# Local attention: keys turned by 32x32 blocks on VectorE and regrouped through DRAM

## The chip, the cores and the metric

The kernel runs on one core of a Trainium2 chip. A core has five engines that work side by side, each through its own queue in order: TensorE (PE in the profile, with its weight loads as PEld), VectorE (DVE), ScalarE (ACT), GpSimd (POOL) and SyncE (SP), which here only issues DMA transfers. Engines wait for each other on semaphores. The metric is the device time of one launch in microseconds.

## The reference, cut to what matters

A transformer of two parts, all in float32. The first part has an attention with relative positions over 16 sequences of 256 tokens, and then six local layers; the second a causal attention and a mixture of experts. The change touches only the attention of the six local layers (16 heads of 64, windows of 32 tokens, each window looking at itself and the one before it):

```python
qkv = x @ Wqkv
q, k, v = split(qkv, 3)                 # then per head
q = l2norm(q) * qs
k = l2norm(k) * ksc
q = q * cos * scale + rotate_half(q) * sin * scale
k = k * cos * inv + rotate_half(k) * sin * inv
sim = einsum('bhwie,bhwje->bhwij', bq, bk2) * 8.0
sim = where(mask, -finfo.max, sim)
attn = softmax(sim, -1)
out = einsum('bhwij,bhwje->bhwie', attn, bv2)
return out @ Wo
```

Since the length of a query is one number for its row and head, dividing by it may come before the rotation, after it, or as a factor of the logits.

## The kernel before

One launch runs four stages in turn: relative attention (`relative_attention`), the six local layers (`local_layers`), causal attention and experts. In the local layers the tokens are cut into tiles of 128 (two per sequence, 32 per layer, 192 in all, `m` in the code). The loop at the end of `local_layers` makes 201 passes; in a pass `at` it issues each entry `(behind, step, ...)` of the table `STEPS` for the tile `at - behind`. So several tiles are in flight, each at a different step, and the order of the table is the order of the instructions: `env.in_order(first)` chains all instructions of PE, ACT, DVE and POOL to the order in which they were written, engine by engine. SP is left out of that, and its transfers are put where the scheduler wants them. Tiles come from pools with a fixed number of buffers (`one`, `two`, `ftwo`, ...); a new tile waits until the last reader of the old one in that buffer has finished. Accumulators are `big` (two buffers of 1024 columns) and `small` (four of 512).

The path of one tile through the steps that matter here:

- `project(m, j)` (L1129; j = 0 is the queries, 1 the keys): two matmuls into a `big` (L1135), squares by ACT (L1146), products with the rotary tables by DVE (L1147, and L1151 on the swapped halves), and their sum by POOL (L1156). It is called for the keys and then for the queries.
- `lengths` (L1160): DVE adds up the squares of queries and keys (L1163).
- `normalise` (L1166): POOL bounds the sums from below (L1169), `power` (L1024) takes the inverse root (ACT L1026, L1027; POOL L1028 to L1031), and POOL multiplies the queries and the keys by it (L1174, twice).
- `turn(m, j)` (L1176): PE turns queries, and in another step keys, 8 blocks of 128x128 each (L1192), ACT copies the result into `a_qT` or `a_kT` (L1193).
- `logits` (L1195): 64 small matmuls into a `big` (L1207); DVE adds the band that masks (L1215) and takes the maximum of each row and head (L1221).
- `exponentials` (L1225): ACT, one head at a time, in three lots of 6, 4 and 6 heads (L1228, each with a read of its accumulator).
- `sums` (L1236): DVE's reciprocal (L1239) and POOL's product with it (L1240). `turn_weights`: DVE turns the weights by 32x32 blocks (L1245).
- `gather` (L1250): matmuls with the tokens (L1260), copied out by ACT (L1268, L1278) and DVE (L1276). `output`: 16 matmuls (L1285) and DVE's sum with the input (L1292).

The feed-forward half of a layer runs once in four passes, for four tiles together (`group`): statistics on DVE (L1316, L1317) with POOL's f_ve behind them (L1319), scaling on DVE (L1331), DVE's product L1374 and sum L1404, POOL's L1397, and their matmuls (L1350, L1366, L1382). `fetch` and `inputs` load a sequence three and two passes ahead (a_xt, L1037 to L1039, and a_xm, L1078 and L1079). POOL also clears edges of fresh tiles (memsets L1040, L1080, L1185).

Of the kernel before, what the change touches and what calls it, by code (L numbers as in the profile page):

```python
# [35 lines left out]
NEG = -1e30  # L36
# [898 lines left out]
def local_layers(tc, I, xa, xb, env):  # L935
# [14 lines left out]
    with ExitStack() as octx:  # L950
# [35 lines left out]
        fou = octx.enter_context(tc.tile_pool(name="a_fou", bufs=4))  # L986

# [15 lines left out]
        x_of, xs_of, kT_of, ffn = {}, {}, {}, {}  # L1003

# [124 lines left out]
        def project(m, j):  # L1129

            i, b, t = where(m)
            ta, tb = tabs[i]["qk"[j]]
            ps = big()
            for c in range(2):
                T.matmul(  # L1135
                    ps[:, c * 512 : (c + 1) * 512],
                    lhsT=xs_of[i, b][:, t, 0:P],
                    rhs=weights[i]["qk"[j]][:, c * 512 : (c + 1) * 512],
                    start=True,
                    stop=True,  # L1140
                )
            ps3 = ps.rearrange("p (h d) -> p h d", h=H)
            u = two.tile([P, H, DH], F32, name=f"a_u{j}")
            r = one.tile([P, H, DH], F32, name=f"a_r{j}")
            sq = one.tile([P, H, DH], F32, name=f"a_sq{j}")
            A.activation(sq, ps3, AF.Square)  # L1146
            V.tensor_mul(u, ps3, bcast(ta[:, t].unsqueeze(1), (P, H, DH)))  # L1147
            swapped = bass.AP(
                ps.tensor, ps.offset + HF, [list(ps.ap[0]), [DH, H], [-HF, 2], [1, HF]]
            )  # L1150
            V.tensor_mul(  # L1151
                r.rearrange("p h (s e) -> p h s e", s=2),
                swapped,
                bcast(tb[:, t].rearrange("p (s e) -> p s e", s=2).unsqueeze(1), (P, H, 2, HF)),
            )
            G.tensor_add(u, u, r)  # L1156
            st[m]["u", j], st[m]["sq", j] = u, sq
            ahead(m, "qk"[j])

        def lengths(m):  # L1160
            ss = two.tile([P, 2, H], F32, name="a_ss")
            for j in range(2):
                V.tensor_reduce(ss[:, j], st[m]["sq", j], AX.X, ALU.add)  # L1163
            st[m]["ss"] = ss

        def normalise(m):  # L1166

            ss = st[m]["ss"]
            G.tensor_scalar_max(ss, ss, 1e-24)  # L1169
            y = two.tile([P, 2, H], F32, name="a_y")  # L1170
            power(ss, y)
            for j in range(2):
                u = st[m]["u", j]
                G.tensor_mul(u, u, bcast(y[:, j].unsqueeze(2), (P, H, DH)))  # L1174

        def turn(m, j):  # L1176

            i, b, t = where(m)
            if j == 0:
                dst = two.tile([P, NP, P], F32, name="a_qT")  # L1180
                st[m]["qT"] = dst
            else:
                if t == 0:
                    kT_of[i, b] = two.tile([P, NP, WIN + S], F32, name="a_kT")
                    G.memset(kT_of[i, b][:, :, 0:WIN], 0.0)  # L1185
                dst = kT_of[i, b][:, :, WIN + t * P : WIN + (t + 1) * P]
            u = st[m]["u", j].rearrange("p h d -> p (h d)")
            for c in range(2):
                ps = small().rearrange("p (c s) -> p c s", c=4)
                for k in range(4):  # L1190
                    o = (4 * c + k) * P
                    T.transpose(ps[:, k, :], u[:, o : o + P], ident)  # L1192
                A.copy(dst[:, 4 * c : 4 * c + 4], ps)  # L1193

        def logits(m):  # L1195
# [7 lines left out]
            for c in range(NP):  # L1203
                for win in range(4):
                    for e in range(2):
                        q0 = WIN * win
                        T.matmul(  # L1207
                            ps[q0 : q0 + WIN, e, c, :],
                            lhsT=qT[DH * e : DH * (e + 1), c, q0 : q0 + WIN],
                            rhs=kT[DH * e : DH * (e + 1), c, t * P + q0 : t * P + q0 + 2 * WIN],  # L1210
                            start=True,
                            stop=True,
                        )
# [7 lines left out]
            V.tensor_reduce(nb, pr, AX.X, ALU.max, negate=True)  # L1221
            den = two.tile([P, H], F32, name="a_den")
            st[m].update(pr=pr, nb=nb, den=den)

        def exponentials(m, h0, h1):  # L1225
            s_ = st[m]
            for h in range(h0, h1):
# [4 lines left out]
                    bias=s_["nb"][:, h : h + 1],  # L1232
                    accum_out=s_["den"][:, h : h + 1],
# [8 lines left out]
        def turn_weights(m):  # L1242

            pT = two.tile([P, H, 2, WIN], F32, name="a_pT")
# [5 lines left out]
        def gather(m):  # L1250
# [21 lines left out]
            for win in (2, 3):  # L1272
                o = g[:, :, WIN * win : WIN * (win + 1)]
                p_ = ps[win].rearrange("p (h q) -> p h q", h=H)
                if win == 2:
                    V.tensor_copy(o, p_)  # L1276
                else:
                    A.copy(o, p_)  # L1278
# [121 lines left out]
        def f_add(i, g):  # L1400
# [7 lines left out]

        STEPS = (
            (2, logits),  # L1410
            (3, sums),
            (0, project, 1),
            (7, group(f_turn)),
            (0, project, 0),
            (3, turn_weights),
            (2, exponentials, 10, 16),
            (1, turn, 0),
            (-2, inputs),
            (4, output),
            (2, exponentials, 0, 4),  # L1420
            (5, group(f_stats)),
            (1, turn, 1),
# [3 lines left out]
            (0, lengths),  # L1426
            (0, fold),
            (5, group(f_power)),
            (3, gather),
            (0, normalise),  # L1430
# [21 lines left out]
        for at in range(N + 9):  # L1452
            for behind, step, *args in STEPS:
                if 0 <= at - behind < N:
# [585 lines left out]
```

## Time and profile before

| what | value |
|---|---|
| time, median of 3 runs | 4092.95 us (4092.0 to 4095.04) |
| span of the profiled execution | 4095.9 us |
| granted TensorE clock over the span | 0.990 |
| PE, DVE, ACT, POOL busy | 98%, 81%, 81%, 68% |
| local layers, about | 720 to 3600 us |
| L1192, turns of queries and keys | 3072 matmuls, 403.0 us busy |
| L1156 / L1174 on POOL, 384 each | 2368 / 1902 ns each |
| L1163 on DVE, 384 | 1201 ns each |

The profile gives one execution, whose own time is not listed beside the runs; its span, from the first to the last instruction, stands for it. A group's line reads: line, engine, operation, output <- inputs, shapes, count, then busy us and mean ns, then the idle time of the engine just before these instructions and who ended it. A line of waits reads: who waited, for whom, us in total, times, longest. A timeline line reads: start us, length us, engine, line, operation, output <- inputs, count, and in brackets the idle time before it. Idle time of an engine that does not set the end costs nothing.

### The profile page before, as it was taken

How to read it: one execution, taken by the hardware profiler on the slowest of the kernel's cores; microseconds unless marked ns; L12 is line 12 of the kernel's file. 1: busy time of each engine (PE TensorE's matmuls, PEld its weight loads, DVE VectorE, ACT ScalarE, POOL GpSimd, SP SyncE). 2: the span in 40 equal slices, each digit the busy share in tenths (PEclk: the TensorE clock that was granted, in tenths of full speed). 3: DMA queues.
4: the chain of work that ended last, by engine and by line, in shares of the span. 5: the costliest groups of instructions: out<-in, count | busy, mean ns of one | idle time of the engine just before them, and what ended most of it. 6: DMA issues, size and time to landing. Idle time of an engine off the chain costs nothing.

```text
span 4095.9 us, 141197 instructions
## 1 busy us (share of the span) xinstructions
PE 4006.0 (98%) x57676; PEld 2910.4 (71%) x57676; DVE 3299.3 (81%) x6445; ACT 3298.4 (81%) x11432; POOL 2774.8 (68%) x3334
## 2 busy tenths in 40 slices
PE   8999999899999999999999999999999999989999
PEld 6888887566777677677767767776776777756666
DVE  5666665788888888888888888888888888869985
ACT  4777776688888888888888888888888888879983
POOL 3333332888888888888888888888888888723221
PEclk9999999899999999999999999999999999999999
DMA  2111112100000000000000000000000000000000
GB/s 70 33 35 35 32 37 60 26 16 20 21 24 19 15 20 20 25 21 20 18 26 15 20 20 21 25 19 15 21 15 25 16 15 15 9 4 2 2 8 22
DMA packets 181812, 90.00 MB, mean 22 GB/s; under 512 B 142493, under 2 KB 173220, under 8 KB 181164
## 3 DMA queue, kind: packets, MB, share of 16 engines
q1 hardware_dynamic: 181164, 80.97, 7.5%
q8 instruction: 455, 7.45, 0.8%
q14 instruction: 193, 1.58, 0.1%
HBM read 38.49 MB, written 6.31 MB: 11 GB/s over the span
## 4 chain that ended last, share of the span: by engine, by line
PE 72%; POOL 6%; ACT 3%; issue 2%; DVE 1%; POOLq 0%; DMA 0%; DVEq 0%; ACTq 0%; SPq 0%
PE small L1285 16%; PE big L1135 13%; PE small L1192 8%; PE big L1260 7%; PE big L1207 5%; PE small L1382 3%; PE small L1366 3%; PE small L1350 3%; PE small L1627 3%; POOL a_u L1174 3%; PE big L1583 3%; PE small L1260 2%; PE small L1643 1%; ACT a_g L1268 1%; POOL a_u L1156 1%
## 5 line engine op out<-in xcount | busy, mean ns | idle before, releaser
L1228 ACT ACTIVATE a_pr<-a_pr,a_nb 128x64 f32<-128x64 f32 x3072 | 1024.1, 338 | 5.8 <-DVE a_nb L1221 5.8
L1156 POOL TENSOR_TENSOR a_u<-a_u,a_r 128x1024 f32<-128x1024 f32 x384 | 900.7, 2368 | 30.7 <-DVE a_r L1151 25.6
L1174 POOL TENSOR_TENSOR a_u<-a_u,a_y 128x1024 f32<-128x1024 f32 x384 | 722.5, 1902 | 15.0
L1285 PE MATMUL small<-a_vo,a_g 128*128 128x128 f32 x6144 | 719.0, 275 | 1.6 <-DVE c_st L1500 1.6
L1285 PEld LDWEIGHTS small<-a_vo,a_g 128*128 128x128 f32 x6144 | 702.5, 192 | 2.6 <-ACT a_g L1278 2.5
L1146 ACT ACTIVATE a_sq<-big 128x1024 f32<-128x1024 f32 x384 | 390.9, 1020 | 263.0 <-PE big L1135 262.7
L1228 ACT ACTIVATION_READ_ACCUMULATOR a_pr<-a_pr,a_nb 128x1 f32 x3072 | 587.8, 191 | 0.0
L1192 PEld LDWEIGHTS small<-ident,a_u 128*128 128x128 f32 x3072 | 350.9, 141 | 141.6 <-POOL a_u L1174 90.4
L1163 DVE TENSOR_REDUCE a_ss<-a_sq 128x16 f32<-128x1024 f32 x384 | 445.9, 1201 | 0.0
L1192 PE MATMUL small<-ident,a_u 128*128 128x128 f32 x3072 | 403.0, 274 | 24.5 <-POOL a_u L1174 21.1
L1135 PE MATMUL big<-w_k,a_xs 128*128 128x512 f32 x768 | 382.9, 621 | 4.6 <-ACT a_xs L1075 4.2
L1240 POOL TENSOR_TENSOR a_pr<-a_pr,a_rd 128x1024 f32<-128x1024 f32 x192 | 365.6, 1904 | 13.0 <-DVE a_rd L1239 13.0
L1135 PE MATMUL big<-w_q,a_xs 128*128 128x512 f32 x768 | 362.0, 594 | 0.6 <-DVE a_r L1151 0.6
L1207 PEld LDWEIGHTS big<-a_kT,a_qT 64*32 64x32 f32 x24576 | 262.7, 105 | 123.4 <-issue 63.8
L1215 DVE TENSOR_TENSOR a_pr<-big,w_band 128x1024 f32<-128x1024 f32 x192 | 234.9, 1223 | 108.6 <-PE big L1207 108.6
L1147 DVE TENSOR_TENSOR a_u<-big,a_tak 128x1024 f32<-128x1024 f32 x192 | 235.1, 1225 | 86.9 <-ACT a_sq L1146 86.9
L1207 PE MATMUL big<-a_kT,a_qT 64*32 64x64 f32 x24576 | 294.6, 226 | 4.7 <-POOL a_kT L1185 4.4
L558 DVE CUSTOM_DVE_ANT_0 r_lg<-big,r_rq 128x256 f32<-128x256 f32 x512 | 186.7, 421 | 132.3 <-PE big L547 81.2
L1268 ACT COPY a_g<-big 128x1024 f32<-128x1024 f32 x192 | 193.6, 1008 | 107.0 <-PE small L1260 106.5
L1135 PEld LDWEIGHTS big<-w_q,a_xs 128*128 128x128 f32 x768 | 142.8, 191 | 163.6 <-issue 126.8
L574 ACT ACTIVATE r_lg<-r_lg,r_nb 128x256 f32<-128x256 f32 x512 | 254.6, 511 | 5.0 <-DVE r_nb L558 5.0
L1609 ACT ACTIVATE c_lg<-c_lg,c_nb 128x256 f32<-128x256 f32 x512 | 255.5, 513 | 0.1
(292 smaller groups left out, 9252.8 us busy)
## 6 DMA issues: line engine op xcount, KB each, us to landing
a_xm<-a_xt SPq DMA_DIRECT2D x96, 96.0 KB
r_dk<-r_rowsk SPq DMA_DIRECT2D x64, 128.0 KB
r_dq<-r_rowsq SPq DMA_DIRECT2D x64, 128.0 KB
f_xt<-xa SPq DMA_DIRECT2D x96, 64.0 KB
f_xt<-xa SPq DMA_DIRECT2D x96, 63.5 KB
a_xt<-xa SPq DMA_DIRECT2D x80, 64.0 KB
a_xt<-xa SPq DMA_DIRECT2D x80, 63.5 KB
w_k<-in_L_ffn_Wqkv_dram SPq DMA_DIRECT2D x6, 512.0 KB
```

What stands on the lines that cost most here:

```text
L1135: T.matmul(ps[:, c * 512 : (c + 1) * 512], lhsT=xs_of[i, b][:, t, 0:P], rhs=weights[i]["qk"[j]][:, c * 512 : (c + 1) * 512], start=True, s ...
L1146: A.activation(sq, ps3, AF.Square)
L1156: G.tensor_add(u, u, r)
L1163: V.tensor_reduce(ss[:, j], st[m]["sq", j], AX.X, ALU.add)
L1174: G.tensor_mul(u, u, bcast(y[:, j].unsqueeze(2), (P, H, DH)))
L1192: T.transpose(ps[:, k, :], u[:, o : o + P], ident)
L1207: T.matmul(ps[q0 : q0 + WIN, e, c, :], lhsT=qT[DH * e : DH * (e + 1), c, q0 : q0 + WIN], rhs=kT[DH * e : DH * (e + 1), c, t * P + q0 : t * ...
L1228: A.activation(s_["pr"][:, h], s_["pr"][:, h], AF.Exp, bias=s_["nb"][:, h : h + 1], accum_out=s_["den"][:, h : h + 1],)
L1240: G.tensor_mul(s_["pr"], s_["pr"], bcast(rd.unsqueeze(2), (P, H, DH)))
L1260: T.matmul(ps[win], lhsT=x[r, t, :], rhs=pT[r, :, o, :], start=(o == 0), stop=(o == 1),)
L1285: T.matmul(ps[:, 0:D], lhsT=st[m]["g"][:, h, :], rhs=weights[i]["vo"][:, h // 2, h % 2, :], start=(h == 0), stop=(h == H - 1),)
L1609: A.activation(lg[:, j], lg[:, j], AF.Exp, bias=nb[:, j : j + 1], scale=-1.0, accum_out=st[b, lc]["den"][:, h : h + 1],)
```

## The change

Keys are no longer turned by PE. DVE turns them by 32x32 blocks (`block_turn`), four DMA transfers write the blocks to DRAM in the order that the logits want, and one reads them back into `a_kT`, now laid out by windows (`keys`). `project` is cut in two: `project` makes the matmuls and squares, `rope` the products with the tables and POOL's sum. The queries are not normalised before the logits: their inverse length multiplies the negated maximum (a DVE multiply in `logits`) and goes into the exponentials as a scale per row. The lengths are taken one side at a time: those of the keys right after their projection, those of the queries at the end of the pass, after POOL has added the two halves of the squares, so that DVE reduces 512 columns instead of 1024. `powers(n)` takes the inverse root for the keys of tile n and the queries of tile n - 1 together. In `gather` ACT takes over the copy that DVE made. `a_pT` has one buffer instead of two. The mask's value is -1e18 instead of -1e30. In the changed program's order DVE's reduction of the queries' squares is L1184, POOL's half add L1182, the turn of the keys L1217.

```diff
--- before
+++ after
-NEG = -1e30
+NEG = -1e18
...
+        held = octx.enter_context(tc.tile_pool(name="a_held", bufs=2, space=DRAM))
...
         def project(m, j):
             i, b, t = where(m)
-            ta, tb = tabs[i]["qk"[j]]
             ps = big()
             for c in range(2):
                 T.matmul(
...
                     start=True,
                     stop=True,
                 )
-            ps3 = ps.rearrange("p (h d) -> p h d", h=H)
+            sq = one.tile([P, H, DH], F32, name=f"a_sq{j}")
+            A.activation(sq, ps.rearrange("p (h d) -> p h d", h=H), AF.Square)
+            st[m]["ps", j], st[m]["sq", j] = ps, sq
+            ahead(m, "qk"[j])
+        def rope(m, j):
+            i, b, t = where(m)
+            ta, tb = tabs[i]["qk"[j]]
+            ps = st[m].pop(("ps", j))
             u = two.tile([P, H, DH], F32, name=f"a_u{j}")
             r = one.tile([P, H, DH], F32, name=f"a_r{j}")
-            sq = one.tile([P, H, DH], F32, name=f"a_sq{j}")
-            A.activation(sq, ps3, AF.Square)
-            V.tensor_mul(u, ps3, bcast(ta[:, t].unsqueeze(1), (P, H, DH)))
+            V.tensor_mul(
+                u,
+                ps.rearrange("p (h d) -> p h d", h=H),
+                bcast(ta[:, t].unsqueeze(1), (P, H, DH)),
+            )
             swapped = bass.AP(
                 ps.tensor, ps.offset + HF, [list(ps.ap[0]), [DH, H], [-HF, 2], [1, HF]]
             )
...
                 bcast(tb[:, t].rearrange("p (s e) -> p s e", s=2).unsqueeze(1), (P, H, 2, HF)),
             )
             G.tensor_add(u, u, r)
-            st[m]["u", j], st[m]["sq", j] = u, sq
-            ahead(m, "qk"[j])
-        def lengths(m):
-            ss = two.tile([P, 2, H], F32, name="a_ss")
-            for j in range(2):
-                V.tensor_reduce(ss[:, j], st[m]["sq", j], AX.X, ALU.add)
-            st[m]["ss"] = ss
+            st[m]["u", j] = u
+        def lengths(m, j):
+            n = m + 1 - j
+            if n not in ss_of:
+                ss_of[n] = two.tile([P, 2, H], F32, name="a_ss")
+                if n in (0, N):
+                    G.memset(ss_of[n][:, n // N], 1.0)
+            sq = st[m].pop(("sq", j))
+            if j == 0:
+                G.tensor_add(sq[:, :, 0:HF], sq[:, :, 0:HF], sq[:, :, HF:DH])
+                sq = sq[:, :, 0:HF]
+            V.tensor_reduce(ss_of[n][:, j], sq, AX.X, ALU.add)
+        def powers(n):
+            ss = ss_of.pop(n)
+            G.tensor_scalar_max(ss, ss, 1e-24)
+            y_of[n] = two.tile([P, 2, H], F32, name="a_y")
+            power(ss, y_of[n])
         def normalise(m):
-            ss = st[m]["ss"]
-            G.tensor_scalar_max(ss, ss, 1e-24)
-            y = two.tile([P, 2, H], F32, name="a_y")
-            power(ss, y)
-            for j in range(2):
-                u = st[m]["u", j]
-                G.tensor_mul(u, u, bcast(y[:, j].unsqueeze(2), (P, H, DH)))
-        def turn(m, j):
-            i, b, t = where(m)
-            if j == 0:
-                dst = two.tile([P, NP, P], F32, name="a_qT")
-                st[m]["qT"] = dst
-            else:
-                if t == 0:
-                    kT_of[i, b] = two.tile([P, NP, WIN + S], F32, name="a_kT")
-                    G.memset(kT_of[i, b][:, :, 0:WIN], 0.0)
-                dst = kT_of[i, b][:, :, WIN + t * P : WIN + (t + 1) * P]
-            u = st[m]["u", j].rearrange("p h d -> p (h d)")
+            u = st[m]["u", 1]
+            G.tensor_mul(u, u, bcast(y_of[m][:, 1].unsqueeze(2), (P, H, DH)))
+        def turn(m):
+            dst = two.tile([P, NP, P], F32, name="a_qT")
+            st[m]["qT"] = dst
+            u = st[m]["u", 0].rearrange("p h d -> p (h d)")
             for c in range(2):
                 ps = small().rearrange("p (c s) -> p c s", c=4)
                 for k in range(4):
                     o = (4 * c + k) * P
                     T.transpose(ps[:, k, :], u[:, o : o + P], ident)
                 A.copy(dst[:, 4 * c : 4 * c + 4], ps)
+        def block_turn(m):
+            u = st[m]["u", 1]
+            ub = one.tile([P, 4, NP * WIN], F32, name="a_ub")
+            V.transpose(
+                ub.rearrange("p e x -> p (e x)"),
+                bass.AP(u.tensor, u.offset, [list(u.ap[0]), [HF, 4], [P, NP], [1, HF]]),
+            )
+            o = st[m]["held"] = held.tile([P, 4, NP * WIN], F32, name="a_rows")
+            for w in range(4):
+                nc.sync.dma_start(
+                    o.rearrange("(e d) w x -> d e w x", e=4)[:, :, w],
+                    ub[WIN * w : WIN * (w + 1)],
+                )
+        def keys(m):
+            i, b, t = where(m)
+            if t == 0:
+                kT_of[i, b] = two.tile([P, 1 + 4 * NT, NP * WIN], F32, name="a_kT")
+                G.memset(kT_of[i, b][:, 0], 0.0)
+            nc.sync.dma_start(kT_of[i, b][:, 1 + 4 * t : 5 + 4 * t], st[m].pop("held"))
         def logits(m):
...
                         T.matmul(
                             ps[q0 : q0 + WIN, e, c, :],
                             lhsT=qT[DH * e : DH * (e + 1), c, q0 : q0 + WIN],
-                            rhs=kT[DH * e : DH * (e + 1), c, t * P + q0 : t * P + q0 + 2 * WIN],
+                            rhs=kT[
+                                DH * e : DH * (e + 1),
+                                4 * t + win : 4 * t + win + 2,
+                                WIN * c : WIN * (c + 1),
+                            ],
                             start=True,
                             stop=True,
                         )
...
             )
             nb = two.tile([P, H], F32, name="a_nb")
             V.tensor_reduce(nb, pr, AX.X, ALU.max, negate=True)
+            V.tensor_mul(nb, nb, y_of[m + 1][:, 0])
             den = two.tile([P, H], F32, name="a_den")
             st[m].update(pr=pr, nb=nb, den=den)
...
                     s_["pr"][:, h],
                     AF.Exp,
                     bias=s_["nb"][:, h : h + 1],
+                    scale=y_of[m + 1][:, 0, h : h + 1],
                     accum_out=s_["den"][:, h : h + 1],
                 )
...
         def turn_weights(m):
-            pT = two.tile([P, H, 2, WIN], F32, name="a_pT")
+            pT = one.tile([P, H, 2, WIN], F32, name="a_pT")
             V.transpose(
                 pT.rearrange("p h o q -> p (h o q)"), st[m]["pr"].rearrange("p h k -> p (h k)")
             )
...
             for win in (2, 3):
                 o = g[:, :, WIN * win : WIN * (win + 1)]
                 p_ = ps[win].rearrange("p (h q) -> p h q", h=H)
-                if win == 2:
-                    V.tensor_copy(o, p_)
-                else:
-                    A.copy(o, p_)
+                A.copy(o, p_)
             st[m]["g"] = g
         def output(m):
...
         STEPS = (
+            (1, block_turn),
             (2, logits),
             (3, sums),
+            (7, group(f_turn)),
             (0, project, 1),
-            (7, group(f_turn)),
+            (0, lengths, 1),
             (0, project, 0),
+            (0, powers),
+            (0, rope, 1),
+            (0, normalise),
+            (0, rope, 0),
             (3, turn_weights),
             (2, exponentials, 10, 16),
-            (1, turn, 0),
+            (1, turn),
             (-2, inputs),
+            (1, keys),
             (4, output),
             (2, exponentials, 0, 4),
             (5, group(f_stats)),
-            (1, turn, 1),
             (8, group(f_sum)),
             (-3, fetch),
             (8, group(f_gate)),
-            (0, lengths),
             (0, fold),
+            (0, lengths, 0),
             (5, group(f_power)),
             (3, gather),
-            (0, normalise),
             (9, group(f_out)),
             (6, group(f_scale)),
             (2, exponentials, 4, 10),
...
         inputs(0)
         for at in range(N + 9):
             for behind, step, *args in STEPS:
-                if 0 <= at - behind < N:
+                if 0 <= at - behind < N + (step is powers):
                     step(at - behind, *args)
         env.in_order(first)
```

More of the change, by code (lines that the diff above doesn't have):

```diff
@@ L1003, in local_layers @@
         x_of, xs_of, kT_of, ffn = {}, {}, {}, {}
+        ss_of, y_of = {}, {}
         def where(m):
```

## The prediction

> **What bounds the kernel now.** First the busy times of the page, then its chain of work that ended last.
>
> ```profile
> PE 4006.0 (98%) x57676; PEld 2910.4 (71%) x57676; DVE 3299.3 (81%) x6445; ACT 3298.4 (81%) x11432; POOL 2774.8 (68%) x3334
> ...
> PE 72%; POOL 6%; ACT 3%; issue 2%; DVE 1%; POOLq 0%; DMA 0%; DVEq 0%; ACTq 0%; SPq 0%
> ```
>
> TensorE is busy nearly always, and most of the chain runs on it. The change lies in the local layers alone (from 720 to 3600 us), so I read that stage by itself in the busy times by stretch (columns: stretch, length, then busy us of PE, PEld, DVE, ACT, POOL, then the granted clock):
>
> ```profile
> 1000.00:3500.00 2500.00, 2485.73 (x35599) 1770.64 (x35599) 2145.43 (x2726) 2118.80 (x7480) 2089.51 (x2333) 1.00 0.08 19
> ```
>
> PE 99%, POOL 84%, DVE 86%. The stage's period: L1245 runs once a pass, first at 766.2 us and last at 3597.3 us, 191 intervals, 14.82 us each. Per pass POOL is busy 0.836 x 14.82 = 12.4 us and idle 2.4 us. So PE bounds, and POOL has little room. What POOL does in one pass, from the timeline:
>
> ```profile
> 2174.62 1.90 POOL L1240 TENSOR_TENSOR a_pr<-a_pr,a_rd 128x1024 f32<-128x1024 f32 x1
> 2176.49 4.69 POOL L1156 TENSOR_TENSOR a_u<-a_u,a_r 128x1024 f32<-128x1024 f32 x2
> 2181.11 0.19 POOL L1080 MEMSET a_xm<- 32x128 f32 x1
> 2181.39 0.28 POOL L1169 TENSOR_SCALAR a_ss<-a_ss 128x32 f32<-128x32 f32 x1
> 2182.94 0.25 POOL L1028 TENSOR_TENSOR a_ss<-a_ss,a_y 128x32 f32<-128x32 f32 x1 [1.26 <-ACT a_y L1027]
> 2183.27 0.25 POOL L1029 TENSOR_TENSOR a_ss<-a_ss,a_y 128x32 f32<-128x32 f32 x1
> 2183.61 0.22 POOL L1030 TENSOR_SCALAR a_ss<-a_ss 128x32 f32<-128x32 f32 x1
> 2183.91 0.25 POOL L1031 TENSOR_TENSOR a_y<-a_ss,a_y 128x32 f32<-128x32 f32 x1
> 2184.24 3.76 POOL L1174 TENSOR_TENSOR a_u<-a_u,a_y 128x1024 f32<-128x1024 f32 x2
> 2187.96 1.90 POOL L1240 TENSOR_TENSOR a_pr<-a_pr,a_rd 128x1024 f32<-128x1024 f32 x1
> ```
>
> From one L1240 to the next POOL stands still once, 1.26 us, for ScalarE. Today nothing that VectorE does early in a pass waits for the end of POOL's pass: DVE's reductions (L1163) feed POOL, and what POOL ends with goes to PE. That is what the change alters. The DVE rows from which I price it (by shape; mean ns behind the busy us):
>
> ```profile
> L1163 DVE TENSOR_REDUCE a_ss<-a_sq 128x16 f32<-128x1024 f32 x384 | 445.9, 1201 | 0.0
> ...
> L1245 DVE STREAM_TRANSPOSE a_pT<-a_pr 128x1024 f32<-128x1024 f32 x192 | 237.1, 1235 | 6.6 <-POOL a_pr L1240 6.6
> ...
> L1276 DVE COPY a_g<-small 128x512 f32<-128x512 f32 x191 | 131.2, 687 | 129.9 <-PE small L1260 126.0
> ...
> L1239 DVE RECIPROCAL a_rd<-a_den 128x16 f32<-128x16 f32 x192 | 46.7, 243 | 9.4 <-ACT a_pr L1228 9.4
> ```
>
> **The change by parts, per pass.** *PE* loses the 8 turns of the keys (L1192): the chain in order of time has 8 of them at 0.87 us. 14.82 - 0.87 = 13.95 us would be its new period. *ACT* loses two copies a_kT (0.58 each) and gains one copy a_g (0.59, L1278), and each exponential takes a scale per row; were that 0.1 us dearer in all 16 (no row shows it; between nothing and one more 0.19 us accumulator read each), ACT pays 1.6 us, which lies in the slack shown below. *DVE* loses the copy L1276 (0.69) and half of one reduction (0.6), and gains a 32x32 turn and a 128x16 multiply: total about even. *POOL* loses one L1174 (1.90), gains a half-width add on the squares. By busy time everything gets better; by order it does not.
>
> **The new ring.** In the changed program's order DVE runs, one after the other: reduce the queries' squares (pass n), turn the keys (pass n+1), add the band, maximum, multiply, reciprocal. The first waits for POOL's half-width add, which is the last of POOL's large operations in pass n. And POOL's first operation of pass n+1, the product with a_rd, waits for that reciprocal. Engines run their queues in order, so this is a closed ring, once per pass:
>
> DVE leg. Handoff 0.08 (L1163 ended at 2167.86, POOL's L1169 began at 2167.94). Reduce half: 0.60, half of 1.20 (bounds 0.25, the 128x16 row, and 1.20). Turn: 1.18 start to start (L1245 at 2176.91, next at 2178.11, 1.20); its input is read in runs of 32, and L1151, which reads so too, takes 1.215 against 1.225 for L1147, which does not. Add to maximum 1.25 (2169.39 to 2170.64). Maximum to a dependent one 1.25. Multiply 0.17 (bounds 0 and 0.25). Reciprocal 0.24, handoff 0.08. Sum **4.85**.
>
> POOL leg. Product 1.87 start to start. L1169 to the next large operation, with ACT free, 2.2 (first pass: L1169 at 734.4, L1174 at 736.6). Rope add of the keys with a dependent successor 2.37 + 0.08 = 2.45. Normalise 1.87. Rope add of the queries 2.33. Half add: from 715 ns at 256 elements (L1397) and 2368 at 1024 (L1156), a line gives 1.27 at 512 (bounds 0.72 and 1.90). Sum **11.99**.
>
> Ring 16.84 us in a pass without feed-forward. What else stands in it, per four passes: on DVE between the reduction and the turn L1331 x4 1.10, L1374 x3 2.1, L1404 x2 0.75, together 0.99 a pass; on POOL ahead of the half add L1397 x2 1.40, f_ve 0.2, and memsets (0.45 and 0.19 in two passes), together 0.72. **18.55 us.**
>
> *Beside it.* PE has 13.95 us for 18.55. ACT ends its last exponentials about 12.9 us after a reciprocal (2.95 to start, then 2.0 + 1.1 + 1.35 to 7.4, a wait for the gather to 8.7, then 2.2 + 2.0) and the next reciprocal needs them at 16.6. The statistics (L1316, L1317) fall into DVE's wait. *Keys through DRAM:* four writes and one read on SP. Nearest row: r_perm to r_rows and back, first write at 255.3, POOL free to go on at 265.8, so 10.5 us; the logits come one ring less 1.4 us after the turn, 15.4. It hides; if it took twice as long, see the rivals. SP's other issues ahead of them (a_xm, a_xt, 0.5 to 0.7 each, one of 2.94) wait for gathers two passes old and cost under 5 us of that.
>
> *The clock.* PE now waits for project q until the add has emptied the logits' accumulator (1.65 us ahead of the reciprocal's end), some 3 us after project k in two of four passes. The trace shows what a gap does: PE idle 2.88 us until 767.58, then the clock 0.57 from 768 to 772; idle 2.19 until 3625.66, then 0.50 from 3628 to 3632. Project q (1.75 us) then takes 3.5, its square ends 3.0 us after the reciprocal, and the Ln that POOL waits for was due at 2.3: 0.7 us in half of the passes, 0.35 (bounds 0 and 0.7). **18.90 us.** [...]
>
> [...]
>
> *Sum.* (18.90 - 14.82) x 191 = +779 us. The profiled span of 4095.9 becomes 4875; it lies 0.07% above the median of 4092.95, so **4870 us**.
>
> **Rivals.**
> 1. *PE stays the bound* (the other side). One mechanism: if POOL's leg and DVE's leg overlap, because the ring is not closed as I read it, the period is PE's 13.95 and the time 4093 - 191 x 0.87 = 3927. It decides from a ring under 13.95, which is 2.9 us less than the bare sum. For: PE 99% busy now. Against: every term but three is a measured row, and these three at their lowest take off 1.1 us. 0.06.
> 2. *The DRAM trip is late.* From 15.4 us on logits wait; at 21 us (twice the row) the period is 22.4, 5540 us. Against: 10.5 us, and the DMA share of the stage is 0.08. 0.03.
> 3. *The clock stays low.* From 3992 to 4008 it read 0.62 and 0.50 after a gap of 2.37 us. If this held over two thirds of a pass, PE needs 13.95 + 9 = 23 us, 5650. Against: the same work recovered within 4 us at 772. 0.05.
> 4. *The ring opens partly* and the time is within 0.2%, about what a measurement of this kernel can tell from no change: 0.01.
>
> The forecast, the ring, has 0.85. Range: unknown terms at their lows together are 18.90 less 0.55 + 0.35 + 0.17 + 0.35 = 17.5, at their highs 0.63 + 0.60 + 0.08 + 0.35 more = 20.6, and handoffs may be 0.3 either way. All at one end is rare; taking three quarters of each way (1.42 and 1.66, each with 0.3) gives 17.6 to 20.4, 4625 to 5160. That leaves out the rivals and a few in a hundred. Slower 0.93, same 0.01, faster 0.06.
>
> **What would show it.** In the profile after: POOL's product with a_rd waiting for DVE's reciprocal some 4 to 6 us a pass, about 900 us in all, and DVE's reduction of a_sq waiting for POOL some 3 to 4 us a pass; PE busy near 80% or filled by a clock below 1; the turn of the keys at about 1.24 us; the half add at 1.27; the granted clock of the stage below 1.00; the period between two turns of the weights 18.9 us. I am wrong if PE is still 99% busy at full clock, if the logits wait for a DMA, or if the half add or turn costs twice its price.

## The result and the profile after

The changed kernel takes **4787.39 us** (median of four runs, 4786.05 to 4790.6) against 4093.99 for the kernel before in the same comparison: ratio 1.1695 [1.1679, 1.1712], slower. The forecast was 4870, the range 4625 to 5160. Line numbers from here on are those of the changed kernel: the half-width add is L1182, the reduction L1184, the turn of the keys L1217, their writes and read L1223 and L1234, POOL's product L1287, the turn of the weights L1292. Lines of an experiment carry the numbers of that experiment's own kernel.

The busy times of its page and the shares of its chain that ended last:

```profile
PE 4067.0 (85%) x56140; PEld 2768.6 (58%) x56140; DVE 3286.8 (69%) x6637; ACT 3505.3 (73%) x11242; POOL 2656.4 (55%) x3341
...
POOL 32%; DVE 24%; PE 19%; issue 7%; ACT 3%; DMA 0%; DVEq 0%; POOLq 0%; SPq 0%; ACTq 0%
```

PE was 98% busy and 72% of the chain; now every engine has idle time, and the chain runs on POOL and DVE. That is how a ring can look in a profile: no engine is full, and yet the time is longer. The local stage by itself (stretch, length, busy us of PE, PEld, DVE, ACT, POOL, granted clock, DMA share, GB/s):

```profile
1000.00:4000.00 3000.00, 2463.63 (x33223) 1594.95 (x33221) 2064.05 (x2801) 2225.98 (x7073) 1921.36 (x2260) 0.96 0.26 73
```

PE 82%, DVE 69%, ACT 74%, POOL 64%. The turn of the weights L1292 first runs at 782.0 and last at 4290.3 us: 191 intervals of **18.37 us**, where 18.90 were forecast and 14.82 stood before. The longest waits of the stage (who, for whom, us in total, times, longest), and three short ones that matter below:

```profile
DVE a_ss L1184 <- POOL a_sq L1182: 1070.2, 192, 7.6
POOL a_pr L1287 <- DVE a_rd L1286: 1028.1, 192, 8.3
...
POOL a_ss L1030 <- ACT a_y L1029: 146.8, 193, 1.4
...
ACT a_y L1028 <- POOL a_ss L1189: 140.2, 156, 5.7
...
PE big L1248 <- DMA a_kT<-a_rows: 9.7, 1, 9.7
```

The first two are the two halves of the ring, once in each of 192 passes: DVE stands 5.6 us for the half add, and POOL 5.4 us for the reciprocal. One turn of the ring can be read from two timelines. POOL's leg, from its product to the half add, in a pass without feed-forward:

```profile
2525.81 1.91 POOL L1287 TENSOR_TENSOR a_pr<-a_pr,a_rd 128x1024 f32<-128x1024 f32 x1 [5.71 <-DVE a_rd L1286]
2527.80 0.29 POOL L1189 TENSOR_SCALAR a_ss<-a_ss 128x32 f32<-128x32 f32 x1
2528.76 0.25 POOL L1030 TENSOR_TENSOR a_ss<-a_ss,a_y 128x32 f32<-128x32 f32 x1 [0.67 <-ACT a_y L1029]
...
2529.95 2.36 POOL L1168 TENSOR_TENSOR a_u<-a_u,a_r 128x1024 f32<-128x1024 f32 x1
2532.38 1.90 POOL L1196 TENSOR_TENSOR a_u<-a_u,a_y 128x1024 f32<-128x1024 f32 x1
2534.24 2.37 POOL L1168 TENSOR_TENSOR a_u<-a_u,a_r 128x1024 f32<-128x1024 f32 x1
2536.55 0.19 POOL L1082 MEMSET a_xm<- 32x128 f32 x1
2536.71 1.25 POOL L1182 TENSOR_TENSOR a_sq<-a_sq 128x512 f32<-128x512 f32 x1
2542.65 1.91 POOL L1287 TENSOR_TENSOR a_pr<-a_pr,a_rd 128x1024 f32<-128x1024 f32 x1 [4.69 <-DVE a_rd L1286]
```

and DVE's leg, which fills that last gap of 4.69 us:

```profile
2538.00 0.69 DVE L1184 TENSOR_REDUCE a_ss<-a_sq 128x16 f32<-128x512 f32 x1 [5.34 <-POOL a_sq L1182]
2538.60 1.23 DVE L1217 STREAM_TRANSPOSE a_ub<-a_u 128x1024 f32<-128x1024 f32 x1
2539.76 1.19 DVE L1260 TENSOR_TENSOR a_pr<-big,w_band 128x1024 f32<-128x1024 f32 x1
2540.98 1.22 DVE L1266 TENSOR_REDUCE a_nb<-a_pr 128x16 f32<-128x1024 f32 x1
2542.23 0.18 DVE L1267 TENSOR_TENSOR a_nb<-a_nb,a_y 128x16 f32<-128x16 f32 x1
2542.33 0.25 DVE L1286 RECIPROCAL a_rd<-a_den 128x16 f32<-128x16 f32 x1
```

Product to product is 2542.65 - 2525.81 = **16.84 us**, the forecast's bare ring to the hundredth, of which POOL's leg is 12.15 (forecast 11.99; 0.16 of it is the memset) and DVE's 4.69 (forecast 4.85). The operations that no row of before had (busy us, mean ns behind it):

```profile
L1274 ACT ACTIVATE a_pr<-a_pr,a_nb,a_y 128x64 f32<-128x64 f32 x3072 | 1311.3, 434 | 1.3 <-DVE a_nb L1267 1.3
L1182 POOL TENSOR_TENSOR a_sq<-a_sq 128x512 f32<-128x512 f32 x192 | 242.0, 1260 | 0.0
L1217 DVE STREAM_TRANSPOSE a_ub<-a_u 128x1024 f32<-128x1024 f32 x192 | 236.9, 1234 | 0.0
L1184 DVE TENSOR_REDUCE a_ss<-a_sq 128x16 f32<-128x512 f32 x192 | 131.7, 686 | 1070.2 <-POOL a_sq L1182 1070.2
```

The half add costs 1.26 us (forecast 1.27), the turn 1.23 (1.18 to 1.24), the halved reduction 0.69. An exponential with a scale for each row takes 434 ns where one without took 338 (L1228 of before): 0.096 us each, 1.5 us a pass, close to the 0.1 that the forecast allowed. The logits wait for the keys from DRAM once in the whole stage, for 9.7 us (the last line of the waits).

### The profile page after: what moved, and what is told of

It reads as the page before. It is cut to its first block, busy times and chain, and to the rows that moved or that the text cites. A ratio compares the mean times of both kernels' runs of the same rounds, so it can differ in the third digit from the quotient of the medians.

```text
span 4788.8 us, 139636 instructions
## 1 busy us (share of the span) xinstructions
PE 4067.0 (85%) x56140; PEld 2768.6 (58%) x56140; DVE 3286.8 (69%) x6637; ACT 3505.3 (73%) x11242; POOL 2656.4 (55%) x3341
## 4 chain that ended last, share of the span: by engine, by line
POOL 32%; DVE 24%; PE 19%; issue 7%; ACT 3%; DMA 0%; DVEq 0%; POOLq 0%; SPq 0%; ACTq 0%
POOL a_u L1168 14%; POOL a_pr L1287 5%; DVE a_ub L1217 4%; DVE a_pr L1260 4%; DVE a_nb L1266 4%; POOL a_sq L1182 4%; PE big L1136 3%; POOL a_u L1196 3%; PE small L1676 2%; PE big L1632 2%; PE small L1426 2%; DVE a_r L1163 2%; DVE a_u L1155 2%; DVE a_ss L1184 2%; PE big L1307 2%
## 5 line engine op out<-in xcount | busy, mean ns | idle before, releaser
L1274 ACT ACTIVATE a_pr<-a_pr,a_nb,a_y 128x64 f32<-128x64 f32 x3072 | 1311.3, 434 | 1.3 <-DVE a_nb L1267 1.3
L1184 DVE TENSOR_REDUCE a_ss<-a_sq 128x16 f32<-128x1024 f32 (+1 forms) x384 | 355.5, 926 | 1089.3 <-POOL a_sq L1182 1070.2
L1287 POOL TENSOR_TENSOR a_pr<-a_pr,a_rd 128x1024 f32<-128x1024 f32 x192 | 365.7, 1905 | 1028.1 <-DVE a_rd L1286 1028.1
L1168 POOL TENSOR_TENSOR a_u<-a_u,a_r 128x1024 f32<-128x1024 f32 x384 | 905.3, 2357 | 0.1
L1136 PE MATMUL big<-w_q,a_xs 128*128 128x512 f32 x768 | 427.1, 683 | 217.8 <-DVE a_pr L1260 217.5
L1274 ACT ACTIVATION_READ_ACCUMULATOR a_pr<-a_pr,a_nb,a_y 128x1 f32 x3072 | 594.4, 193 | 0.0
L1307 PE MATMUL big<-a_pT,a_xm 32*128 32x512 f32 x768 | 228.5, 667 | 252.0 <-DVE a_pT L1292 250.3
L1136 PE MATMUL big<-w_k,a_xs 128*128 128x512 f32 x768 | 401.1, 647 | 9.6 <-ACT a_xs L1077 4.2
L1196 POOL TENSOR_TENSOR a_u<-a_u,a_y 128x1024 f32<-128x1024 f32 x192 | 365.2, 1902 | 15.1
L1307 PE MATMUL small<-a_pT,a_xm 32*128 32x512 f32 x768 | 279.5, 673 | 25.1 <-ACT f_hT L1401 24.9
L1207 PEld LDWEIGHTS small<-ident,a_u 128*128 128x128 f32 x1536 | 196.0, 150 | 121.8 <-issue 117.0
L1307 PE MATMUL small<-a_pT,a_xt 32*128 32x512 f32 x768 | 258.2, 644 | 0.0
```

The lines of the kernel that those rows point to most:

```text
L1136: T.matmul(ps[:, c * 512 : (c + 1) * 512], lhsT=xs_of[i, b][:, t, 0:P], rhs=weights[i]["qk"[j]][:, c * 512 : (c + 1) * 512], start=True, s ...
L1184: V.tensor_reduce(ss_of[n][:, j], sq, AX.X, ALU.add)
L1196: G.tensor_mul(u, u, bcast(y_of[m][:, 1].unsqueeze(2), (P, H, DH)))
L1274: A.activation(s_["pr"][:, h], s_["pr"][:, h], AF.Exp, bias=s_["nb"][:, h : h + 1], scale=y_of[m + 1][:, 0, h : h + 1], accum_out=s_["den" ...
L1287: G.tensor_mul(s_["pr"], s_["pr"], bcast(rd.unsqueeze(2), (P, H, DH)))
L1307: T.matmul(ps[win], lhsT=x[r, t, :], rhs=pT[r, :, o, :], start=(o == 0), stop=(o == 1),)
```

## The experiments

**Theory:** the ring of DVE's and POOL's legs sets the pass. **Rivals:** PE at a lower clock, and the trip through DRAM. All edits are made on the changed kernel. To place effects I use, beside the times, mean lengths from reciprocal to reciprocal between 2000 and 2600 us, by the feed-forward part that lies in the pass (four kinds in turn). A difference in time divided by 191 is its worth a pass.

| kernel | ratio to before | gated unit | output | scale | plain | mean |
|---|---|---|---|---|---|---|
| before | 1 | 18.21 | 15.60 | 12.79 | 13.17 | 14.94 |
| after | 1.1695 | 20.70 | 17.85 | 18.13 | 17.12 | 18.45 |
| e1_full | 1.0985 | 20.03 | 16.47 | 15.92 | 14.99 | 16.85 |
| e2_late | 1.1456 | 21.07 | 18.46 | 16.91 | 15.19 | 17.91 |
| e3_pe | 1.1245 | 20.47 | 16.78 | 17.01 | 16.20 | 17.62 |
| e4_trip | 1.3082 | 20.70 | 19.64 | 26.32 | 18.32 | 21.25 |
| e5_fill | 1.1774 | 20.58 | 18.12 | 18.37 | 17.61 | 18.67 |
| e7_half | 1.1259 | 20.21 | 17.75 | 17.03 | 15.08 | 17.52 |
| e11_full_turn | 1.0854 | 20.11 | 16.50 | 15.99 | 14.17 | 16.69 |
| e13_all | 1.0708 | 20.03 | 16.47 | 15.87 | 13.27 | 16.41 |
| e15_after_turn | 1.1701 | 20.80 | 17.82 | 18.14 | 17.24 | 18.50 |
| e18_turn_end | 1.0647 | 20.12 | 16.53 | 14.80 | 14.01 | 16.37 |
| e19_scale | 1.1074 | 19.84 | 16.49 | 14.01 | 18.70 | 17.26 |
| e20_copy | 1.1032 | 19.41 | 16.04 | 14.54 | 18.73 | 17.18 |

**e1_full: no half add, so no closed ring.**

```diff
-            if j == 0:
-                G.tensor_add(sq[:, :, 0:HF], sq[:, :, 0:HF], sq[:, :, HF:DH])
-                sq = sq[:, :, 0:HF]
             V.tensor_reduce(ss_of[n][:, j], sq, AX.X, ALU.add)
```

> POOL's half add of the queries' squares is dropped and DVE reduces all 1024 columns at the same place in its queue, so that this reduction waits for ACT's square only. Ring theory: the ring through the last large operation of POOL is open; the next longest is product, powers, rope add of the keys, normalise, turn, add, maximum, reciprocal, 8.4 + 4.25 = 12.65 us, under PE's 13.95, so the pass falls from 18.4 to between 14.0 and 15.0 us, some 4050 us (3950 to 4150), with ACT (13.6 us busy a pass) and DVE (13.1) close behind PE. Rival, the trip of the keys through DRAM or the lower clock sets the pass: nothing is gained, 4790 us, a little more for the longer reduction.

4496.57 us, 1.0985 [1.0965, 1.1005]: 291 us less, 1.52 us a pass, although DVE now does twice the reduction. The ring is a cause, but the pass falls to 16.85, not near PE's 13.95: a second limit lies close below. Its waits, in the stage:

```profile
POOL a_pr L1284 <- DVE a_rd L1283: 942.3, 192, 9.4
PEld big L1304 <- issue: 394.0, 414, 5.3
PE big L1304 <- DVE a_pT L1289: 313.5, 145, 5.1
```

DVE's wait for POOL's half add is gone, POOL's for the reciprocal has stayed, and PE's gather (L1304) waits for the turned weights.

**e2_late: the half add stays, its reduction comes one pass later.**

```diff
             if j == 0:
                 G.tensor_add(sq[:, :, 0:HF], sq[:, :, 0:HF], sq[:, :, HF:DH])
-                sq = sq[:, :, 0:HF]
+                st[m]["half"] = sq[:, :, 0:HF]
+                return
             V.tensor_reduce(ss_of[n][:, j], sq, AX.X, ALU.add)
+        def late(m):
+            V.tensor_reduce(ss_of[m + 1][:, 0], st[m].pop("half"), AX.X, ALU.add)
...
             (0, lengths, 1),
+            (1, late),
```

> POOL's half add stays where it is; DVE's reduction of the queries' squares moves to the next pass, behind the reduction of the keys' squares and ahead of the inverse root that needs it, so that nothing on DVE before the reciprocal waits for POOL's half add. Same instructions as the changed kernel. Ring theory: 14.0 to 14.8 us a pass, 3950 to 4090 us. Rival, DRAM trip or clock: 4790 us.

4690.6 us, 1.1456 [1.1438, 1.1473]: only 97 us less, 0.51 a pass. The plain pass gains 1.9 us, but those with the gated unit and the output lose 0.4 and 0.6. Two new costs show; neither was priced by a run of its own. ACT's next square waits for this reduction, since `a_sq` has one buffer (388.3 us over 191 times). And DVE, freed from waiting, now scales the feed-forward's input just beside POOL's long adds. The scaling line by its statistics (ns min/median/max) in this kernel:

```profile
L1380 DVE TENSOR_SCALAR f_xt<-f_xt,f_mv,f_rs x192: 326/1461/2806, 879.2 to 4219.0; 128x128 f32<-128x128 f32 x192
```

and in the changed one:

```profile
L1375 DVE TENSOR_SCALAR f_xt<-f_xt,f_mv,f_rs x192: 326/340/760, 891.5 to 4319.4; 128x128 f32<-128x128 f32 x192
```

The same instruction takes four times as long at the median. In one pass four of them fill 5.48 us from 2532.65, while POOL runs its product L1201 (2532.14 to 2534.04) and its adds L1168 (2534.00 to 2536.35) and L1182 (2536.73 to 2538.04); the next DVE operation starts at 2538.05. That POOL's work holds the scaling up is my reading of these rows; by what means is not shown.

**e3_pe: keys turned by PE as before, into the new layout; no transfers, `keys` three steps later in the table, the rest as changed.**

```diff
-            (1, block_turn),
...
+            for c in range(2):
+                ps = small().rearrange("p (c w s) -> p c w s", c=4, w=4)
+                for k in range(4):
+                    o = (4 * c + k) * P
+                    T.transpose(ps[:, k], u[:, o : o + P], ident)
+                A.copy(
+                    kT_of[i, b][
+                        :, 1 + 4 * t : 5 + 4 * t, 4 * WIN * c : 4 * WIN * (c + 1)
+                    ].rearrange("p w (c s) -> p c w s", c=4),
+                    ps,
+                )
```

> The keys go back to PE (8 turns and two ACT copies into the new layout, no transfers), everything else as changed, the order of the reductions too. Ring theory: the turn on DVE, 1.18 us, leaves the ring, so 18.37 - 1.18 = 17.2 us a pass, 4560 us, although PE and ACT have more to do. Rival, PE or its clock sets the pass: 0.87 us more a pass, 4950 us. Rival, the DRAM trip sets it: back to PE's bound, about 4090 us.

4603.19 us, 1.1245 [1.1228, 1.1261]: 0.96 us a pass *faster* than the changed kernel, though PE gets back 8 turns (its busy share in the stage rises from 82% to 90%). What the ring loses is the turn on DVE, 1.2 us. A PE-bound kernel would have lost time, and one that waits for DRAM would have come back to 4090. The run takes out the transfers together with the turn; as the logits of the changed kernel wait for them only once, the gain is put down to the turn's place on DVE.

**e4_trip: every write and read of the keys issued twice.**

```diff
+            for n in range(2):
                 for w in range(4):
                     nc.sync.dma_start(
                         o.rearrange("(e d) w x -> d e w x", e=4)[:, :, w],
                         ub[WIN * w : WIN * (w + 1)],
                     )
...
+            for n in range(2):
                 nc.sync.dma_start(kT_of[i, b][:, 1 + 4 * t : 5 + 4 * t], o)
```

> Each of the four writes of the turned keys and the read is issued twice, the second time with the same bytes. Ring theory: the trip has over 5 us to spare, 4790 us within 0.5%. Rival, the trip sets the pass: at least four more issues of 0.4 us and one more transfer of 512 KB ahead of the logits, 2 to 5 us a pass, 5150 to 5700 us.

5356.49 us, 1.3082 [1.3063, 1.3102]. I had held that over 5 us were to spare; this costs 2.98 us a pass, most of it in the pass with the scaling (26.32 for 18.13). The logits now wait:

```profile
PE big L1251 <- DMA a_kT<-a_rows: 623.1, 92, 13.5
```

and SP's queue shows where the time goes in one such pass (the length is that of the issue):

```profile
2516.07 0.46 SPq L1237 DMA_DIRECT2D a_kT<-a_rows  x1
...
2519.80 0.34 SPq L1237 DMA_DIRECT2D a_kT<-a_rows  x1
...
2521.69 3.47 SPq L1041 DMA_DIRECT2D a_xt<-xa  x1
2525.20 4.88 SPq L1224 DMA_DIRECT2D a_rows<-a_ub  x8
```

The second read is issued 3.7 us after the first, then an input transfer holds the queue for 3.5 us, and only then come the eight writes. So the trip is hidden in the changed kernel, but not when doubled: in the changed kernel's pass four writes go out from 2539.86, the read only at 2546.79, behind 4.8 us of other issues, and PE starts the logits on these keys at 2557.69.

**e5_fill: the projection of the keys done twice on PE, to keep its clock up.**

```diff
+            if j == 1:
+                for c in range(2):
+                    T.matmul(
+                        ps[:, c * 512 : (c + 1) * 512],
+                        lhsT=xs_of[i, b][:, t, 0:P],
+                        rhs=weights[i]["qk"[j]][:, c * 512 : (c + 1) * 512],
+                        start=True,
+                        stop=True,
+                    )
```

> PE makes the keys' projection twice into the same accumulator, so that most of its wait ahead of the queries' projection is filled with matmuls of the same result. My term for the clock (0.35 us a pass, because a slow projection of the queries delays ACT's Ln): up to 0.35 us less, 4720 us. If the term is nothing: 4790 us within 0.5%, since Ln waits for POOL's maximum. If PE set the pass: 0.9 to 1.8 us more, 4960 us or above.

4819.82 us, 1.1774 [1.1757, 1.1792]. The stretch 1000 to 4000 of this kernel:

```profile
1000.00:4000.00 3000.00, 2638.99 (x33532) 1683.96 (x33530) 2065.70 (x2777) 2220.29 (x7032) 1913.55 (x2246) 0.99 0.25 72
```

The clock is 0.99 instead of 0.96, and the time 32 us longer, a little above the 4790 within 0.5% that I gave for a term of nothing. The lower clock costs nothing that filling it gives back.

**e7_half: the half add ahead of the queries' rotary add on POOL.**

```diff
             (0, normalise),
+            (0, half),
             (0, rope, 0),
```

> Same instructions as the changed kernel; POOL's half add moves ahead of its rope add of the queries, so that this add (2.33 us) and the memsets and L1441 behind it (0.72) run beside DVE's leg of the ring. Ring theory alone: 18.37 - 2.33 - 0.72 = 15.3 us a pass, 4200 us. With the second obstacle that the first two runs point to (PE's gather waits for the turned weights, which DVE now reaches 2.4 us later behind the turn of the keys and the reduction): no better than the run with the full reduction, 16.9 us a pass, 4450 to 4550 us.

4610.54 us, 1.1259 [1.1242, 1.1276]; better than after by 0.93 a pass, worse than both figures that I gave. DVE's wait for the half add falls as the ring says:

```profile
POOL a_pr L1291 <- DVE a_rd L1290: 819.3, 192, 9.8
...
DVE a_ss L1183 <- POOL a_sq L1188: 374.2, 192, 4.1
```

and the plain pass loses 2.0 us, where the add and the memset that leave its ring are 2.5; the pass with the scaling gives 1.1, that with the gated unit only 0.5 and that with the output 0.1. So the ring theory comes near in the plain pass alone, and the sum over passes was too hopeful.

**e11_full_turn and e13_all: the second limit.** On e1, first the turn of the weights ahead of the queries' products; then also the clearing of a_kT's edge (`edge`, taken out of `keys`) ahead of POOL's long run; e11 is without that first line.

```diff
+            (1, edge),
             (0, rope, 1),
             (0, normalise),
-            (0, rope, 0),
             (3, turn_weights),
+            (0, rope, 0),
```

> The run with the full reduction, and the turn of the weights moved on DVE from behind the rotation of the queries to ahead of it, 2.3 us earlier. If the gather's wait for the turned weights is the second obstacle: 2 us less a pass than with the full reduction alone (16.9), 14.8 to 15.3, 4080 to 4190 us. Rival, the second obstacle is DVE's reciprocal ring or the scaling that POOL locks out: 4400 us or more.

> As the last, and the clear edge of the keys' tile is written by POOL ahead of its rope adds instead of behind them (PE's logits waited for it at the first tile of a sequence, about 2 us in every second pass in the changed kernel). If that wait is on the path once the ring is open: 0.3 to 0.8 us less a pass than the last, 4000 to 4100 us; if not, the same within 0.5%.

e11: 4443.49 us, 1.0854 [1.0836, 1.0872], 53 us less than e1 where I expected some 2 us a pass, and on the side of the rival (4400 or more). The gather's wait did fall, from 313.5 us to 50.4, but most of it had covered other waits: it was long, and not the limit. e13: 4383.17 us, 1.0708 [1.0692, 1.0724], 60 us less again, at the low end of what I expected. The plain pass is now 13.27 us, as before the change (13.17); the pass with the gated unit has not moved since e1.

**e15_after_turn: the same early turn of the weights, ring closed.** The control to e11.

> The changed kernel with nothing but the turn of the weights moved 2.3 us earlier on DVE; the ring stays closed. Ring theory: PE's gather waits less and nothing is gained, 4790 us within 0.5% (the pass with the gated unit, whose chain runs through the gather, may give up to 0.2 us in the mean). Rival, PE's wait for the turned weights is what the change costs: 2 us less a pass, 4400 us.

4791.69 us, 1.1701 [1.1684, 1.1719]: nothing gained. Its two largest waits (1000 to 4000 us) are those of the changed kernel:

```profile
DVE a_ss L1184 <- POOL a_sq L1182: 879.6, 161, 7.6
POOL a_pr L1287 <- DVE a_rd L1286: 869.6, 162, 7.5
```

The same edit is worth 53 us with the ring open and nothing with it closed. While a ring is closed, only what stands in it counts.

**e18_turn_end: e13, and the turn of the keys at the end of the pass before.**

```diff
-            (1, block_turn),
...
             (0, lengths, 0),
+            (0, block_turn),
```

> As the run with the full reduction, the early turn of the weights and the early memset (passes by kind 20.0, 16.5, 15.9, 13.3 us between reciprocals, mean 16.4), and the turn of the keys moves from the head of the next pass to the end of its own, ahead of the feed-forward's work on DVE. If what is left is a second ring through DVE's feed-forward products, the turn of the keys and the logits' add: 1.2 us less in the passes with those products, some 0.7 in the one with the scaling, mean 15.5, 4210 us. If that ring does not pass the turn: 4380 us within 0.5%.

4359.11 us, 1.0647 [1.0631, 1.0663]: 24 us less than e13, not some 170, and within 0.5% of the 4380 for a ring that does not pass the turn. The passes with the products and the output do not fall in the table, the scale pass gains 1.1 and the plain one loses 0.7. The scale pass's gain fits the scaling, not a ring: four scalings in e13 take

```profile
2105.46 3.21 DVE L1376 TENSOR_SCALAR f_xt<-f_xt,f_mv,f_rs 128x128 f32<-128x128 f32 x4
```

beside a POOL add from 2105.45 to 2107.81, and in e18, where the turn stands ahead of them and the same add (from 2099.70 to 2102.06) is half over when they start,

```profile
2100.95 1.96 DVE L1376 TENSOR_SCALAR f_xt<-f_xt,f_mv,f_rs 128x128 f32<-128x128 f32 x4
```

In the changed kernel, after POOL's adds, they take 1.11. This is the best version found, and still slower than before.

**e19_scale and e20_copy: scaling moved away from POOL's adds; then one copy of the gather back on DVE.** e19 takes f_scale ahead of the reciprocal and f_turn behind `(1, turn)`.

```diff
             (2, logits),
+            (7, group(f_scale)),
             (3, sums),
-            (7, group(f_turn)),
...
             (1, turn),
+            (7, group(f_turn)),
...
-            (6, group(f_scale)),
```

> As the last, and DVE's scaling of the feed-forward's input moves to the head of the next pass, ahead of the reciprocal, where POOL stands idle (in the runs with an open ring four of these took up to 5.5 us together instead of 1.1, beside POOL's adds). If the two engines lock each other out: that pass falls by 1 to 1.5 us, mean 0.3 less, 4150 us. If the scaling was slow for another reason: no change, or 0.3 us more a pass for its 1.1 us ahead of the reciprocal.

> As the last, and DVE makes one of the gather's three copies again, as before the change. ACT has 13.7 us a pass, in the pass with the gated unit 17.6, and its last exponentials end the wait for the reciprocal: 0.6 us less on ACT, 0.2 to 0.5 less a pass, 4060 to 4110 us. If ACT does not set the pass: the same or slower by up to 0.6.

e19: 4535.22 us, 1.1074 [1.1055, 1.1092], 176 us *more* than e18. The scaling is short again (four in 1.11 us, 0.85 less than in e18), and its pass falls by 0.8 to 14.0, but the plain pass rises to 18.7. The waits of e19 name it:

```profile
PEld small L1330 <- ACT a_qT L1205: 234.4, 45, 5.3
...
DVE xa L1337 <- PE small L1330: 228.5, 46, 6.0
```

With f_turn in its new place the output's small accumulator comes free only after ACT's copies of the turned queries, 5 us in one pass of four, and DVE behind it waits too. So this run prices the scaling in its own pass and not in the sum. e20: 4517.34 us, 1.1032 [1.1016, 1.1049], 0.09 us a pass better than e19 where 0.2 to 0.5 was expected; it takes 0.4 off the gated unit's and the output's passes, and adds 0.5 to the scale pass.

**What stays.** e18 is 1.4 us a pass above before, and why is open. In the pass with the gated unit (stretch, length, busy PE, PEld, DVE, ACT, POOL), before:

```profile
2064.78:2083.00 18.22, 18.06 (x213) 11.28 (x212) 13.74 (x17) 15.91 (x48) 15.55 (x17) 1.00 0.07 17
```

and in e13, where e1's rows read nearly the same:

```profile
2125.35:2145.21 19.86, 18.47 (x205) 9.96 (x204) 14.27 (x17) 17.39 (x47) 11.47 (x14) 1.00 0.24 65
```

The pass is 1.64 us longer, ACT works 1.48 us more, and 16 exponentials at 0.096 us are 1.54. PE no longer fills the pass (1.4 us idle), and POOL has much less to do. The dearer exponentials can be a part of what is left, but not all of it. Before, DVE's first product of the gated unit starts 12.69 us after the reciprocal,

```profile
2077.47 1.61 DVE L1374 SCALAR_TENSOR_TENSOR f_hT<-small,w_b,f_hT 128x512 f32<-128x512 f32 x2 [0.53 <-PE small L1366]
```

and in e13 13.45 us after it, 0.76 later, in a stretch that holds ten of the exponentials. The other 0.88 lie between this product and the next reciprocal, where the turn of the keys now stands:

```profile
2138.80 1.61 DVE L1419 SCALAR_TENSOR_TENSOR f_hT<-small,w_b,f_hT 128x512 f32<-128x512 f32 x2 [4.35 <-PE small L1411]
...
2141.48 1.24 DVE L1214 STREAM_TRANSPOSE a_ub<-a_u 128x1024 f32<-128x1024 f32 x1
```

e18 takes the turn out of that stretch: between 1000 and 3200 us most of its passes with the gated unit take 19.49 us, most of e13's 19.86; some of over 20.8 in each raise the means in the table. This is argued from rows and not tested: no kernel with the ring open and the old exponentials was run, and the other kinds of pass were not split like this.

## Why the prediction was right, and where it was off

1. *The new ring.* Right in its parts and its sum: 16.84 us forecast, 16.84 measured. The half add's price by a line through two other widths (1.27) and the turn's by its neighbour in shape (1.18 start to start) were good to 2%. That the sum agrees to the hundredth is chance: one memset of 0.16 us, which the forecast counts with the rest, stands in the measured pass, and DVE's leg is 0.16 shorter than forecast. e1 opens the ring and gains 1.5 us a pass, e3 and e7 shorten it and gain 0.9, and e15 changes what lies outside it and gains nothing.
2. *What else stands in it.* 1.71 us a pass were forecast for the feed-forward. Measured, 18.37 - 16.84 = 1.53 is all there is beyond the bare ring, or 1.69 with that memset. In the four passes from 2525.81 to 2599.03 us the rows between the reduction and the turn take 1.98, 0.66, 1.02 and 0 us, 0.92 a pass (forecast 0.99), and those ahead of the half add 1.80, 0.48, 0.44 and 0.16, 0.72 a pass (forecast 0.72). In all four DVE waits for the half add and POOL for the reciprocal.
3. *The clock: the step that failed.* "Project q ... its square ends 3.0 us after the reciprocal ... 0.7 us in half of the passes, 0.35." The clock did fall (0.96 in the stage), but in 156 of 193 cases ACT's Ln (L1028) waited for POOL's own maximum, so there it was not late; POOL waited for ACT 0.76 us a pass against 0.67 in the quiet pass above, at most 0.1 us more. e5 put the clock back to 0.99 and gained nothing. So the slow PE was free beside the closed ring. This term is most of the 0.53 us a pass by which the forecast was high; (18.90 - 18.37) x 191 is 101 us, and the profiled span is 86 below the forecast's.
4. *The waits it named.* POOL's for the reciprocal, 1028 us (about 900 forecast); DVE's for the half add 5.6 us a pass, forecast 3 to 4. PE 82% busy, forecast near 80. "By busy time everything gets better" was not so: ACT's rose from 3298 to 3505 us, as the forecast's own 1.6 us a pass for the exponentials implies.
5. *Keys through DRAM hide.* Right: one wait of 9.7 us. e4, with every write and read doubled, costs 2.98 us a pass, near the 3.5 (22.4 - 18.90) that the second rival put on a trip of twice the length; what was wrong is the expectation ahead of e4, that such a trip would still hide.
6. *The first rival's price was wrong*, and nothing in the forecast tested it: with the ring open it gave PE's 13.95 us. e1, e11, e13 and e18 open it and find 16.4 to 16.9 (means of the table), above the 14.94 of before. So the ring alone does not explain the whole loss; it is the highest of several limits. Taking it away gives back 42% of the 693 us (291, e1), with the later ordering edits 62% (428, e18). What holds the remaining 38% is not shown.

## What to carry to other kernels

Where instructions run in a written order, follow each new wait forward until it returns to the engine that it started from; if it does within one pass, add up that circle, because the new period cannot be shorter, whatever the busy shares say. Busy time taken off the fullest engine is worth only the distance to the next limit, so ask what the pass would be with each limit gone, and do not price the favourable case by the fullest engine alone. A long wait in a profile may cover others: the gather's 313 us was worth 53.

## What the runs showed of the hardware

An exponential of 128x64 with a scale for each row takes 434 ns against 338 with a bias alone, with almost no spread (423 to 468 against 327 to 366). A scaling of 128x128 by VectorE (f_xt onto itself) takes 0.34 us at the median in the changed kernel, where it stands behind GpSimd's adds, and in e2, beside them, 1.46 at the median and up to 2.8. On SP's queue a single issue of a_xt (L1041) held those behind it for 2.84 us in the changed kernel and 3.47 in e4, and in one pass of the changed kernel the read of the turned keys went out 6.9 us after the first of their writes (2539.86 to 2546.79).
